# Four chained transformer layers on one core: later fp4 weights, a packed tile written twice, and a planner that counts a slow TensorE after a pause

## The chip, the cores and the metric

The kernel runs on one core of one Trainium2 chip, as a single program. The metric is the device time of that program in microseconds. Three runs of the kernel before gave 2689.86, 2690.91 and 2692.45 us, so the median is 2690.91 us.

## What is computed

The input `x` has 8 sequences of 1024 rows of 256 numbers, in float32. Four blocks follow each other, each of the form `x = x + block(layernorm(x))`:

```python
x = x + _L0_attn_ref(_layernorm(x), ...)   # linear attention with 16 heads, then a 256-1024-256 MLP with gelu
x = x + _L0_ffn_ref(_layernorm(x), ...)    # 256-1024-256 MLP with relu
x = x + _L1_attn_ref(_layernorm(x), ...)   # softmax attention, 256 wide, over the 1024 rows of a sequence
x = x + _L1_ffn_ref(_layernorm(x), ...)    # gated MLP, 704 wide
```

The last block rounds both its activations and its three weight matrices to a 4-bit grid in groups of 16:

```python
scale = jnp.maximum(jnp.max(jnp.abs(xb), axis=-1, keepdims=True) / 6.0, 1e-12)
q = _GRID[jnp.searchsorted(_MID, jnp.abs(xb / scale))] * jnp.sign(xb / scale) * scale
```

The linear attention forms running sums along the sequence (`cumsum`), sums products over the 16 numbers of a head, and multiplies vectors of 16 numbers by one number per head and position.

## The kernel before

**Tiling.** A chunk is 128 rows, a group (the code says flow) is four chunks, so a sequence has two flows and the program has 16, numbered p = 0 to 15. Each flow passes through linear attention (`linear_group`, `linear_span` at line 919, `linear_chunk` at 1079), then through the two MLPs of layer 0 (`dense`, 1269), then layernorms (`norms_1`, `norms_2`). Once both flows of a sequence are through, its eight chunks pass through softmax attention and the fp4 MLP (`soft_chunk`, 1429). Different flows are at different stages at the same time: the linear attention of flow p runs among the MLP work of flow p - 1 and the soft chunks of earlier sequences.

**Who sets the order.** Every part of the work is a Python generator that yields what it needs next. The class `Plan` (line 63) keeps a small model of the machine while the program is being written: when each engine is free, when each tile is done. `Plan.run` (267) always takes the part whose next step could start soonest, and among equals the one with the lowest due number `at`, which is counted in flows. `Plan.took` (157) charges each step a cost in this model; the TensorE cost is 1.68e-3 us per column of a matmul, and a DMA is charged at 160 GB/s on one shared `rings` time. Every instruction is recorded by the class `Queue`, whose call is line 308; so nearly all instructions of the profile have the line L308, and they are told apart by their tiles. `add_manual_dep` pins the order on each engine to the order in which the plan wrote it. Nothing is decided at run time: what the plan wrote first on an engine runs first on it.

**DMAs.** All DMAs are issued by SyncE (SP) in one order. An SP instruction whose tile isn't ready holds up all DMAs written after it. The MLP weights stream through five buffers `w_ff` of 256 KB (`W_FF = 5`, `load_weights` at 1314): one MLP step reads one buffer, with two matmuls of `half` (the first layer) and, up to two steps later, two matmuls into the accumulator (`w_ff,hidden`). The two DMAs that refill a buffer can only be issued when its last matmul is done.

**The spread.** In linear attention one number per head and position has to be multiplied into 16 rows. The numbers are packed: `flow` and later `scale` are [128, 128] tiles whose row 32 t + h holds head h at the 128 positions of chunk t. `spread` (763) writes such a tile to DRAM as `flat`, 32 rows of 512 numbers, and reads it back so that every head's row lands on 16 partitions: 4 tiles of [128, 512] for `flow`, 2 for `scale`. This is done in the flows p = 1 to 15; flow 0 works in halves and uses matmuls in its place (`spread_near`, 785). On the way back the source pattern is 8 rows, each 16 times, of 512 numbers:

```python
ap=[[GT, 8], [0, DH], [1, width]],
```

What follows the spread of `flow` on VectorE (DVE): for each of four tiles a product with `k` or `q`, a running sum (`prod<-one,carry_w,spread`) and another product. Then come the head sums on TensorE (`prod,hsum`), the division (`div`), and the packed tile `scale`, whose spread is multiplied into `q`; only then can the chunks of the flow start (`qz`).

**The fp4 weights.** `fp4_weights` (645) loads 18 pieces of the three matrices (`w_raw`), rounds each on DVE and ScalarE (ACT) with the helper `fp4` (604), transposes it on TensorE and copies it to `wgT`, `wuT` or `wdT`. Its due number is `at = 0.9 + 2.2 * i / 18` for piece i. It may start once the MLPs have begun (`count["stage"] == 4`). The soft chunks need all pieces before their first product with `wgT`.

Of the kernel before, what the change touches and what calls it, by code (L numbers as in the profile page):

```python
# [9 lines left out]
F32 = mybir.dt.float32  # L10
# [6 lines left out]
P = 128  # L17
D = 256
H = 16
DH = D // H  # L20
# [10 lines left out]
GT = G * P  # L31
# [31 lines left out]
class Plan:  # L63
# [12 lines left out]
    def __init__(self, tc, nc):  # L76
        self.tc, self.nc = tc, nc
        self.free = {}
        self.done = {}
        self.by = {}  # L80
        self.banks = []
        self.live = {}
        self.slots = {}
        self.kind = {}
        self.size = {k: v[0] for k, v in TILES.items()}
        self.spare = False
        self.used = {}
        self.held = set()
        self.kept = set()
        self.last = {}  # L90
        self.act_set = 0
        self.tiled = False
        self.parts = []
        for name in ("tensor", "vector", "scalar", "gpsimd", "sync"):
            setattr(self, name, Queue(self, name))
# [61 lines left out]
    def took(self, queue, op, args, kw):  # L157

        aps = [x for x in list(args) + list(kw.values()) if isinstance(x, bass.AP)]
        outs = [kw["out"] if "out" in kw else aps[0]]  # L160
        if kw.get("accum_out") is not None:
            outs.append(kw["accum_out"])
        size = 1
        for ap in aps:
            n = 1
            for d in ap.shape[1:]:
                n *= d
            size = max(size, n)
        after = 0.06
        if queue == "tensor":  # L170
            size = 1
            for d in outs[0].shape[1:]:
                size *= d
            cost = size * (0.84e-3 if op == "transpose" else 1.68e-3)
            tiled = op == "matmul" and (kw["lhsT"].shape[-1] <= 32 or kw["lhsT"].shape[0] <= 32)
            if tiled:
                cost *= 0.25
            if tiled != self.tiled:
                cost += 0.2
            self.tiled = tiled  # L180
            after = 0.2
        elif queue == "vector":
            each = {"reciprocal": 6.2e-3, "tensor_tensor_scan": 2.15e-3}.get(op, 1.05e-3)
            cost = 0.15 + each * size
            if op == "tensor_scalar" and outs[0].dtype == BF16:
                cost = 0.16 + 0.26e-3 * size
        elif queue == "scalar":
            cost = (0.16 if op == "copy" else 0.26) + 0.82e-3 * size
            for x in args:
                if not isinstance(x, bass.AP) and self.SETS.get(x, self.act_set) != self.act_set:  # L190
                    self.act_set = self.SETS[x]
                    cost += 1.3
        elif queue == "gpsimd":
            cost = 0.55 + 0.7e-3 * size
            if op in ("tensor_scalar", "iota"):
                cost = 0.22
            elif op == "memset":
                cost = 0.1 + 0.9e-3 * size
        else:
            cost = 0.4  # L200
        start = self.free.get(queue, 0.0)
        for ap in aps:
            name = ap.tensor.name
            if self.by.get(name) != queue:
                start = max(start, self.done.get(name, 0.0))
            if name not in self.done and name in self.held:
                start = max(start, self.used[name])
        end = start + cost
        if queue == "sync":
            n = 4e-6 / 160e-3  # L210
            for d in outs[0].shape:
                n *= d
            self.free["rings"] = max(self.free.get("rings", 0.0), end) + n
            after = self.free["rings"] - end + 1.8
        self.free[queue] = end
        for ap in outs:
            self.done[ap.tensor.name] = end + after
            self.by[ap.tensor.name] = queue
        for ap in aps:
            name = ap.tensor.name  # L220
            self.used[name] = max(self.used.get(name, 0.0), end + after)
            if queue != "tensor" and name not in self.kept:
                self.held.discard(name)
# [11 lines left out]
    def pe(self, *tiles, **kw):  # L235
        return self.need("tensor", tiles, **kw)

    def dve(self, *tiles, **kw):
        return self.need("vector", tiles, **kw)

    def act(self, *tiles, **kw):
        return self.need("scalar", tiles, **kw)

    def dma(self, *tiles, **kw):
        return self.need("sync", tiles, **kw)
# [81 lines left out]
def block_stack_kernel(ctx: ExitStack, tc: tile.TileContext, a: dict, out: bass.AP):  # L327
# [21 lines left out]
    nc, pe, dve, act, dma = plan, plan.pe, plan.dve, plan.act, plan.dma  # L349
# [9 lines left out]
    hbm = ctx.enter_context(tc.tile_pool(name="hbm", bufs=1, space=bass.MemoryType.DRAM))  # L359
# [10 lines left out]
    def tr_bank():  # L370
        return mm_bank().rearrange("p (k t) -> p k t", k=4)

    def fresh(kind, need, name=None):

        need.fresh = kind
        yield need
        return make(kind, name)
# [151 lines left out]
    for i in (1, 0):  # L529
        nc.sync.dma_start(out=wqkv[i], in_=wqkv_in[i])  # L530
        nc.sync.dma_start(
            out=bqk1[:, 2 * i : 2 * i + 2],
            in_=a[f"L0_attn_b{'qk'[i]}"].rearrange("(k p) -> p k", p=P),
# [111 lines left out]
    def fp4_weights():  # L645
        pieces = []
        for name, dstT in (("L1_ffn_w_gate", wgT), ("L1_ffn_w_up", wuT)):
            for r0, rows in INTER_TILES:
                turns = [(dstT[:, k, r0 : r0 + rows], k * P, P) for k in range(2)]
                pieces.append((a[name][r0 : r0 + rows, :], turns))  # L650
        for n in range(2):
            for c0 in range(0, INTER, D):
                width = min(D, INTER - c0)
                turns = []
                for f0 in range(0, width, P):
                    rows = min(P, width - f0)
                    dst = wdT[:rows, (c0 + f0) // P, n * P : (n + 1) * P]
                    turns.append((dst, f0, rows))
                pieces.append((a["L1_ffn_w_down"][n * P : (n + 1) * P, c0 : c0 + width], turns))
        raws = {}  # L660
        for i, (src, turns) in enumerate(pieces):
            for j in range(i, min(i + 3, len(pieces))):
                if j not in raws:
                    ahead = pieces[j][0]
                    raws[j] = (yield from fresh(
                        "soft",
                        dma(at=0.9 + 2.2 * i / len(pieces), when=lambda: count["stage"] == 4),
                        "w_raw",
                    ))[
                        : ahead.shape[0], : ahead.shape[1]  # L670
                    ]
                    nc.sync.dma_start(out=raws[j], in_=ahead)
            rows, width = src.shape
            raw = raws.pop(i)
            at = 0.9 + 2.2 * i / len(pieces)
            yield dve(raw, at=at)
            yield from fp4(raw, width, rows)
            yield pe(raw, banks=1)
            bank = tr_bank()
            for k, (dst, c0, n) in enumerate(turns):  # L680
                nc.tensor.transpose(bank[:n, k, :rows], raw[:, c0 : c0 + n], ident[:rows, :rows])
            plan.drop(raw)
            yield act(bank)
            for k, (dst, c0, n) in enumerate(turns):
                nc.scalar.copy(dst, bank[:n, k, :rows])
        weights.add("fp4")
# [76 lines left out]
    def spread(packed, tiles):  # L763


        width = packed.shape[0] // 32 * P
        flat = hbm.tile([32, GT], F32, tag="packed", name="packed", bufs=4)
        yield dma(packed)
        nc.sync.dma_start(
            out=flat[:, :width].rearrange("r (t l) -> t r l", l=P), in_=packed  # L770
        )
        out = {}
        for b in tiles:
            t = out[b] = yield from fresh("flow", dma(flat), "spread")
            nc.sync.dma_start(
                out=t[:, :width],
                in_=bass.AP(
                    tensor=flat.tensor,
                    offset=flat.offset + 8 * b * GT,
                    ap=[[GT, 8], [0, DH], [1, width]],  # L780
                ),
            )
        return out
# [22 lines left out]
    def running(out, cur, carry, b, first, last):  # L806
# [19 lines left out]
    count = {  # L826
        "halves": 0,
        "dense": 0,
        "acc": 0,
        "res": 0,  # L830
        "v": 0,
        "scored": 0,
        "attended": 0,
        "linear": 0,
# [787 lines left out]
```

## Time and profile before

| what | value |
|---|---|
| median of the runs before | 2690.91 us (2689.86 to 2692.45) |
| the profiled execution's own time | 2683.94 us |
| its span | 2682.2 us |
| mean granted TensorE clock | 0.991 |
| TensorE matmul busy (PE) | 2597.4 us, 97% of the span |
| VectorE busy (DVE) | 1969.3 us, 73% |
| ScalarE busy (ACT) | 1246.7 us, 46%, of it 308 table loads of 1283 ns |
| GpSimd busy (POOL) | 560.5 us, 21% |
| DMA | 207.00 MB in the kernel's queue, 25.9% of 16 engines |
| DMAs `packed<-flow` and `packed<-scale` | 15 and 15, 64 KB each |
| DMAs `spread<-packed` | 90, 256 KB each |

The profiled execution is 7 us shorter than the median of the timed runs; its durations and its span belong together, so sums are made against it. Times in the views are microseconds from the span's start. PE is the matmul side of TensorE, PEld its weight loads, SPq the DMA-issuing queue of SyncE. A float32 matmul has two records in the trace. In brackets behind a row stands how long the engine was idle before it, and what it waited for. In a table of windows, each engine has its busy time in that window, then come the granted share of the TensorE clock, the busy share of the core's 16 DMA engines, and what they moved.

### The profile page before, as it was taken

What the parts mean: (1) busy time and instruction counts of PE and PEld (TensorE: products, weight loads), DVE (VectorE), ACT (ScalarE), POOL (GpSimd) and SP (SyncE); (2) the same over time, 40 slices, a digit from 0 to 9 for tenths busy, and PEclk for the clock granted to TensorE, in tenths of its full rate; (3) what the DMA queues carried; (4) which work ended last, traced back from release to release, by engine and by line L of the source; (5) the groups of instructions that cost most, each with busy time, mean ns of one, the idle gap of its engine ahead of it and who ended that gap; (6) DMA issues with size and microseconds to landing.
All of it is one profiled execution on the core that took longest, in us unless ns stands there. A gap on an engine that the chain in (4) does not pass through costs nothing.

```text
span 2682.2 us, 45602 instructions
## 1 busy us (share of the span) xinstructions
PE 2597.4 (97%) x16687; PEld 2014.0 (75%) x16687; DVE 1969.3 (73%) x4514; ACT 1246.7 (46%) x2430; POOL 560.5 (21%) x1101
## 2 busy tenths in 40 slices
PE   6999999999999999999999999999999999999997
PEld 4777777777777777777777777777777777787765
DVE  8889687776858668686776858778586776856576
ACT  2443445535455453645536354363635536344343
POOL 1232232221212213122131212212121131212000
PEclk8999999999999999999999999999999999999999
DMA  3334222312223222232322223132231322322100
GB/s 87 107 105 143 89 82 64 108 59 89 73 69 106 66 86 73 69 96 71 91 73 76 80 75 106 52 92 75 70 108 54 98 63 71 89 66 81 41 12 12
DMA packets 282135, 209.92 MB, mean 78 GB/s; under 512 B 23864, under 2 KB 270392, under 8 KB 281912
## 3 DMA queue, kind: packets, MB, share of 16 engines
q1 hardware_dynamic: 281912, 207.00, 25.9%
q8 instruction: 133, 2.18, 0.3%
q14 instruction: 90, 0.74, 0.1%
HBM read 188.17 MB, written 18.74 MB: 77 GB/s over the span
## 4 chain that ended last, share of the span: by engine, by line
PE 80%; DVE 12%; DMA 2%; issue 1%; ACT 1%; POOL 1%; SPq 0%; DVEq 0%; ACTq 0%
PE bank L308 80%; DVE hid L308 2%; DVE prod L308 1%; DVE n L308 1%; DVE ln_st L308 1%; DMA spread<-packed 1%; DVE x_amax L308 1%; DVE u L308 1%; DMA w_ff<-in_L_attn_W_dram 1%; DVE res L308 1%; POOL ln_rstd L308 1%; DVE div L308 1%; DVE e L308 0%; DVE q L308 0%; DVE ln_mv L308 0%
## 5 line engine op out<-in xcount | busy, mean ns | idle before, releaser
L308 PE MATMUL bank<-half,w_ff 128*128 128x256 f32 x2048 | 533.6, 383 | 14.5 <-DMA w_ff<-in_L_ffn_w_dram 6.0
L308 PE MATMUL bank<-w_ff,hidden 128*128 128x256 f32 x2048 | 530.4, 383 | 7.7 <-issue 6.6
L308 PEld LDWEIGHTS bank<-half,w_ff 128*128 128x128 f32 x2048 | 379.4, 191 | 91.4 <-issue 26.6
L308 PEld LDWEIGHTS bank<-w_ff,hidden 128*128 128x128 f32 x2048 | 371.1, 191 | 96.0 <-issue 50.7
L308 ACT ACT_TABLE_LOAD x308 | 395.2, 1283 | 75.2 <-PE bank L308 71.1
L308 POOL TENSOR_SCALAR ln_ve<-ln_mv 128x1 f32<-128x1 f32 x384 | 96.0, 250 | 1320.7 <-DVE ln_mv L308 1299.4
L308 ACT ACTIVATE hidden<-bank,c_L_ffn_b 128x256 f32<-128x256 f32 x256 | 121.1, 473 | 338.0 <-PE bank L308 336.7
L308 PE MATMUL bank<-n2T,qT 128*128 128x512 f32 x512 | 241.4, 594 | 0.9 <-ACT qT L308 0.9
L308 POOL TENSOR_TENSOR ln_rstd<-ln_ve,neghalf 128x1 f32<-128x1 f32 x384 | 229.4, 597 | 32.0
L308 PE MATMUL bank<-vt,probT 128*128 128x256 f32 x1024 | 232.2, 380 | 0.0
L308 PEld LDWEIGHTS bank<-vt,probT 128*128 128x128 f32 x1024 | 193.2, 190 | 30.3 <-issue 3.3
L308 ACT ACTIVATE hidden<-bank,c_L_attn_b 128x256 f32<-128x256 f32 x256 | 121.4, 474 | 177.0 <-PE bank L308 175.4
L308 PE MATMUL bank<-wdT,hqT 128*128 128x256 f32 x768 | 178.0, 382 | 1.8 <-ACT hqT L308 1.8
L308 PE MATMUL bank<-wgT,xqT 128*128 128x352 f32 x512 | 173.4, 461 | 1.1 <-ACT xqT L308 0.9
L308 PE MATMUL bank<-wuT,xqT 128*128 128x352 f32 x512 | 172.4, 459 | 0.0
L308 DVE TENSOR_TENSOR sc<-bank,triu 128x512 f32<-128x512 f32 x256 | 159.4, 679 | 5.3 <-PE bank L308 3.8
L308 PEld LDWEIGHTS bank<-wdT,hqT 128*128 128x128 f32 x768 | 145.4, 191 | 22.8 <-ACT hqT L308 2.8
L308 DVE TENSOR_TENSOR hid<-hid,bank 128x352 f32<-128x352 f32 x118 | 60.9, 516 | 133.8 <-PE bank L308 92.0
L308 POOL TENSOR_TENSOR xr<-xr,b_L_attn_ln_b 128x256 f32<-128x256 f32 x64 | 49.3, 788 | 482.6 <-DMA xr<-in_L_attn_inputs_dram 482.6
L308 PEld LDWEIGHTS bank<-n2T,qT 128*128 128x128 f32 x512 | 93.6, 190 | 69.5 <-issue 62.7
L308 PEld LDWEIGHTS bank<-wuT,xqT 128*128 128x128 f32 x512 | 97.3, 190 | 54.2
L308 PEld LDWEIGHTS bank<-wgT,xqT 128*128 128x128 f32 x512 | 92.6, 190 | 37.0 <-issue 3.8
(214 smaller groups left out, 4384.4 us busy)
## 6 DMA issues: line engine op xcount, KB each, us to landing
w_ff<-in_L_attn_W_dram SPq DMA_DIRECT2D x512, 128.0 KB
w_ff<-in_L_ffn_w_dram SPq DMA_DIRECT2D x512, 128.0 KB
spread<-packed SPq DMA_DIRECT2D x90, 256.0 KB
x<-in_L_attn_inputs_dram SPq DMA_DIRECT2D x64, 128.0 KB
xr<-in_L_attn_inputs_dram SPq DMA_DIRECT2D x64, 128.0 KB
rows<-res SPq DMA_DIRECT2D x64, 128.0 KB
out_dram<-y SPq DMA_DIRECT2D x64, 128.0 KB
rows<-rows SPq DMA_DIRECT2D x56, 128.0 KB
```

The lines of the kernel that those rows point to most:

```text
L308: ins = method(*args, **kw)
```

## The change

Three edits. First, the plan's model: a TensorE step that starts more than 2.0 us after the last one ended makes TensorE cost double until 2.1 us after that start, and DMAs are charged at 250 GB/s in place of 160. Second, the fp4 weight pieces get the due numbers 1.5 to 3.0 in place of 0.9 to 3.0. Third, the packed tile is written to DRAM twice, side by side (`flat` becomes [32, 2, 512]), by two DMAs, and a spread reads 16 rows, each 8 times, in place of 8 rows, each 16 times. The tile that it fills is the same.

```diff
@@ class Plan, __init__
+        self.ran = self.slow = 0.0
@@ class Plan, took
+        if queue == "tensor":
+            if start - self.ran > 2.0:
+                self.slow = start + 2.1
+            if start < self.slow:
+                cost *= 2
+            self.ran = start + cost
         end = start + cost
         if queue == "sync":
-            n = 4e-6 / 160e-3
+            n = 4e-6 / 250e-3
@@ fp4_weights
-                        dma(at=0.9 + 2.2 * i / len(pieces), when=lambda: count["stage"] == 4),
+                        dma(at=1.5 + 1.6 * i / len(pieces), when=lambda: count["stage"] == 4),
...
-            at = 0.9 + 2.2 * i / len(pieces)
+            at = 1.5 + 1.6 * i / len(pieces)
@@ spread
-        width = packed.shape[0] // 32 * P
-        flat = hbm.tile([32, GT], F32, tag="packed", name="packed", bufs=4)
+        flat = hbm.tile([32, 2, GT], F32, tag="packed", name="packed", bufs=4)
         yield dma(packed)
-        nc.sync.dma_start(
-            out=flat[:, :width].rearrange("r (t l) -> t r l", l=P), in_=packed
-        )
+        for e in range(2):
+            nc.sync.dma_start(out=flat[:, e, :].rearrange("r (t l) -> t r l", l=P), in_=packed)
...
             nc.sync.dma_start(
-                out=t[:, :width],
+                out=t,
                 in_=bass.AP(
                     tensor=flat.tensor,
-                    offset=flat.offset + 8 * b * GT,
-                    ap=[[GT, 8], [0, DH], [1, width]],
+                    offset=flat.offset + 8 * b * 2 * GT,
+                    ap=[[GT, 16], [0, DH // 2], [1, GT]],
                 ),
             )
```

## The prediction, written before the result was known

> **What bounds the kernel now.** I read the page's busy times, then the windows of four stages, to see where TensorE isn't full.
>
> ```profile
> core 0: us, PE busy (x) PEld busy (x) DVE busy (x) ACT busy (x) POOL busy (x), PEclk, DMA share, GB/s
> 0.00:84.70 84.70, 59.15 (x472) 44.00 (x473) 68.99 (x185) 25.80 (x62) 19.06 (x50) 0.82 0.29 76
> 84.70:345.00 260.30, 242.21 (x1802) 190.72 (x1801) 214.97 (x510) 111.64 (x259) 77.83 (x143) 0.97 0.39 115
> 345.00:2414.00 2069.00, 2047.18 (x13313) 1593.58 (x13312) 1513.59 (x3425) 1002.59 (x1898) 439.15 (x853) 1.00 0.26 79
> 2414.00:2682.20 268.20, 248.82 (x1105) 185.71 (x1103) 171.75 (x397) 106.63 (x213) 24.42 (x56) 0.99 0.12 37
> ```
>
> The matmuls are the same before and after, so a change can move only TensorE's idle time and the time at a low clock. Idle are 84.7 - 59.15 = 25.6 us at the start, 260.3 - 242.2 = 18.1 us in the ramp, 21.8 us in the long middle (1%), 19.4 us at the end: 85 us in all. Next, the ramp's worst two stretches, and who ended TensorE's waits there (time line of PE, then of SP):
>
> ```profile
> 135.00 2.07 PE L308 MATMUL bank<-half,w_ff 128*128 128x256 f32 x4 [5.72 <-DMA w_ff<-in_L_ffn_w_dram]
> ...
> 230.16 2.08 PE L308 MATMUL bank<-half,w_ff 128*128 128x256 f32 x4 [4.28 <-DMA w_ff<-in_L_attn_W_dram]
> ```
>
> ```profile
> 124.48 2.52 SPq L308 DMA_DIRECT2D spread<-packed  x4
> 127.10 0.88 SPq L308 DMA_DIRECT2D xr<-in_L_attn_inputs_dram  x2
> 128.08 6.32 SPq L308 DMA_DIRECT2D w_ff<-in_L_ffn_w_dram  x6
> ...
> 221.13 2.44 SPq L308 DMA_DIRECT2D spread<-packed  x4
> 223.68 0.91 SPq L308 DMA_DIRECT2D w_ff<-in_L_attn_W_dram  x2
> ```
>
> Both pauses, 10.0 us together, are MLP weights that were issued behind the four spreads of flows 1 and 2. The first pair is issued at 128.08 and lets TensorE go at 135.00, 6.9 us later; a load in an empty queue (`xr`, at 212.10 on the chain that ended last) took 2.06 us. While only spread data is moving:
>
> ```profile
> 224.00:226.00 2.00, 1.08 (x6) 0.44 (x4) 1.90 (x5) 0.30 (x2) 0.12 (x1) 1.00 0.51 196
> ```
>
> half of the 16 DMA engines are busy and they move 196 GB/s. The pauses are followed by half clock:
>
> ```profile
> 131.60:138.40 6.80, 3.40 (x8) 2.77 (x9) 6.62 (x9) 0.47 (x1) 3.88 (x4) 0.50 0.64 159
> 227.20:234.00 6.80, 3.84 (x9) 3.14 (x10) 6.48 (x13) 0.47 (x1) 0.00 (x0) 0.50 0.55 146
> 63.40:73.40 10.00, 7.52 (x22) 5.84 (x23) 6.06 (x17) 2.69 (x7) 2.25 (x8) 0.50 0.01 2
> ```
>
> At half clock the 3.40 and 3.84 us of matmuls cost 1.7 and 1.9 us more than at full clock, the 7.52 us at 63 cost 3.8. DVE is nearly full in the first two (6.62 and 6.48 of 6.8 us). Last, a pause at the start that isn't a DMA's:
>
> ```profile
> 65.88 0.34 PE L308 MATMUL bank<-ident,scale 64*128 64x64 f32 x1 [3.35 <-DVE scale L308]
> ```
>
> **What the Trainium skill says.** "DMA: Bandwidth & Descriptors", section "Why a DMA increments its semaphore by 16 and not by 1": a DMA of this kind runs on the largest k up to 16 engines that divides the slowest dimension of both sides. The spread's source begins with 8 rows: k = 8, which agrees with the DMA share of 0.51 above; with 16 rows k = 16. The packed write begins with 4: k = 4, and stays there. "TensorE: Matmul & The Clock Gate", "Part 1: The HAM clock gate": the clock is halved after an idle window of some 3.4 us and comes back after a busy one; the trace agrees in kind (0.50 in pieces of 6.8 us), but the clock fell here only 1.3 us after the pause at 225.9 began.
>
> **The change part by part.** Sums are against the profiled execution, 2683.94 us; its span of 2682.2 is 1.7 less, and the median of the runs is 7.0 more. I carry the difference over to the median.
>
> *Spread on 16 engines.* Four spreads are 4 x 256 KB = 1.05 MB: 1.05 MB / 196 GB/s = 5.35 us before. On 16 engines at the same rate each, 2.7 us; their issue takes 2.5 us anyway. All that queues behind moves up by 2.65 us. In the built order the weights of MLP steps 16 (flow 1's spread) and 47 (flow 2's) still stand right behind the spreads, and between the first spread and their use lies as much matmul work as before (some 4.9 and 4 us), so the pauses don't vanish: 5.7 - 2.65 = 3.1 and 4.3 - 2.65 = 1.6. In flow 1 the two `xr` loads no longer stand ahead (0.88 us), one `w_raw` does (0.42): 2.6. Bounds: below, both fall to about 1 us (2.06 us landing behind the issue alone); above, nothing is gained if source rows or memory hold the spreads, not their engines.
>
> *Packed row twice.* 30 more issues at 0.57 us on SP, and the copy runs on 4 engines again. The spread waits for both, perhaps 0.9 to 1.5 us longer, and SP's weights wait behind it. The plan puts 3.0 us of matmuls between packed write and spread of flow 2 where it put 2.1, which covers most; I charge 0.4 us in each of the two places: pauses 3.0 and 2.0, gain 2.7 + 2.3 = 5.0 us. In flows 3 to 15 the spreads lie under MLP and soft-chunk matmuls: between 345 and 2414 us TensorE waited 1.9 us in all for a weight (longest 1.1), so nothing is counted there. If that cover is gone, see the third rival.
>
> *Half clock at the two pauses.* With 2 to 3 us they may stay above the point: the 2.24 us pause at 334.6 kept full clock, 3.35 us didn't. Of 1.7 + 1.9 I take 3.0.
>
> *fp4 weights later.* A piece costs DVE 0.41 + 0.17 + 0.25 + 0.42 + 0.22 + 2 x 0.42 + 0.43 = 2.7 us, 18 pieces 49 us. In the built order 9 `w_raw` instructions of DVE stand ahead of flow 1's spread where 27 did: 18 / 5 x 2.7 = 9.7 us of DVE less, and that spread comes some 8 us of matmuls earlier. This relieves the waits for a DVE `n` or `w_raw` at 145 (0.89), 160 (0.74), 221 (0.82) and 225 (0.79): of 3.2 us I take 1.5. The work lands in front of 325, where there is room: DVE is busy 22.5 of the 40 us from 285. It costs nothing there; the last transpose stands 35 us of matmuls ahead of the first product with `wgT`. The loads move on SP too, 18 issues of 0.42 us; none falls between spreads and a late weight except the one counted.
>
> *The plan's half rate.* In the built order the second half of flow 0 changes: its `prod,hsum` comes before the matmuls of chunk 1, and on DVE two `kv` products (0.48) and `u`, its statistics, `u`, `h` (about 1.9) no longer stand ahead of `e`, or do so after it. So `scale` is some 2.5 us earlier at 65.9: gain 2.5 us (bounds 1 and 3.4, the whole pause). Of the 3.8 us at half clock after it I take 0.5. The order reconverges: from flow 5 on the same steps stand within a few us of each other, and of the last 1400 TensorE rows 36 differ, so the end's 19 us stay.
>
> *Table loads.* The built order has 320 where 308 were, 12 x 1.283 = 15.4 us of ACT, which is idle over half the time. At 311 two loads in a row did cost a pause of 1.4. I charge 0.5 us in one of three, 2 us; the ends are 0 and 15.4, and reshuffled work in the middle may add 3 us either way.
>
> Sum: 5.0 + 3.0 + 1.5 + 2.5 + 0.5 - 2 = 10.5; I round up to 12, since a ramp with fewer pauses feeds the middle's 21.8 us better too. 2690.9 - 12 = 2679.
>
> **Rivals.** (1) The ramp closes: pauses to about 1 us and no half clock: 8 + 3.6 + 3.2 of waits, 3.4 + 3.8 at the start: 22 us, 2669. For it: issue takes as long as the data on 16 engines. Against it: the weights stand as close behind the spreads as before. (2) Spreads aren't held by engines, since each 2 KB row is read many times from one place: the pauses stay, table loads take back the start's gain: 2688 to 2691. For it: nothing but the doubt that 392 GB/s are to be had; against it: 0.51 at 196. This includes the change not doing what it says. (3) Slower: SP's order. Behind `packed` SP waits some 1.5 us longer, 30 times, and weights queue there. In steady flows the shortest distance from a weight's issue to its use behind a pair of spreads is 3.5 us of matmuls, against 2.06 us of landing. If the longer wait exceeds this slack by 1 us in flows 3 to 15, 13 x 2 x 1 = 26 us are lost against 12 won: 2705; it decides from 0.7 us. Against it: faster spreads shorten that same landing.
>
> **Numbers.** Chances: forecast (2673 to 2685) 0.56, ramp closes (2664 to 2672) 0.14, nothing gained (2686 to 2693) 0.20, SP slower (over 2696) 0.10. 0.2% is 5.4 us, about what a measurement of this kernel can tell from no change: faster, below 2685.5, is 0.56 + 0.14 + 0.02 = 0.72; slower 0.10; same 0.18. The range is 2664 to 2693: it leaves out the third rival and some tails.
>
> **What would show it.** Spreads: a DMA share near 1 and over 300 GB/s behind the four issues, in place of 0.51 and 196. Pauses before `half,w_ff` at flows 1 and 2 of 1 to 3 us and at most one piece of half clock after 80. `ident,scale` near 63. The middle's idle time within 4 us of 21.8. I am wrong if the pauses keep their length, if new ones stand behind `packed`, or if the middle moves more than the ramp.

## The result and the profile after

The changed kernel took 2683.17 us (median of 6 runs, 2680.7 to 2688.15) against 2691.68 us before (6 runs): ratio 0.9973, 95% interval 0.9963 to 0.9984. A second, longer comparison (21 runs against 41) gave 2683.32 against 2689.54 us, ratio 0.9976 (0.9970 to 0.9983). By the ratios the change gains 6.5 to 7.3 us (by the medians 6.2 and 8.5) of the 12 forecast.

The two profiled executions show almost none of this: 2683.53 us (span 2681.8) after, 2683.94 before. The profiled execution before was quicker than any of the 41 timed runs of its kernel. In the longer comparison the mean granted clock was 0.9906 after and 0.9892 before. By an estimate from these means, 0.0014 x 2690 = 3.8 us of the gain is time lost at half clock, which a pair of single profiles doesn't show reliably. The rest is idle time of TensorE. The windows of the four stages, after (columns as in the prediction):

```profile
core 0: us, PE busy (x) PEld busy (x) DVE busy (x) ACT busy (x) POOL busy (x), PEclk, DMA share, GB/s
0.00:84.70 84.70, 61.21 (x470) 44.87 (x471) 69.19 (x183) 25.38 (x61) 20.20 (x51) 0.80 0.29 76
84.70:345.00 260.30, 244.71 (x1816) 192.66 (x1815) 205.86 (x508) 117.64 (x266) 74.50 (x141) 0.99 0.39 113
345.00:2414.00 2069.00, 2044.74 (x13302) 1592.06 (x13301) 1524.56 (x3429) 1009.10 (x1904) 465.31 (x853) 1.00 0.28 80
2414.00:2681.80 267.80, 250.23 (x1104) 187.22 (x1103) 171.57 (x397) 106.53 (x213) 25.43 (x56) 0.99 0.12 37
```

Window less PE busy is idle time: 23.5 at the start (25.6 before), 15.6 in the ramp (18.1), 24.3 in the middle (21.8), 17.6 at the end (19.4). In all 81.0 in place of 84.9: 3.9 us less, and with the 3.8 us of clock 7.7, which is about the measured gain.

Where the ramp waits now (time line of PE, after):

```profile
65.27 0.25 PE L315 MATMUL bank<-ident,scale 64*128 64x64 f32 x1 [2.64 <-DVE scale L315]
124.66 1.10 PE L315 MATMUL bank<-half,w_ff 128*128 128x256 f32 x4 [3.15 <-DMA w_ff<-in_L_ffn_w_dram]
131.62 0.43 PE L315 MATMUL bank<-prod,hsum 128*32 128x128 f32 x8 [1.62 <-DVE prod L315]
151.70 1.17 PE L315 MATMUL bank<-qz,k 32*128 32x256 f32 x16 [2.54 <-ACT qz L315]
225.38 0.44 PE L315 MATMUL bank<-ident,w_raw 128*128 128x128 f32 x2 [2.57 <-DVE w_raw L315]
249.41 0.33 PE L315 MATMUL bank<-ident,scale 128*128 128x128 f32 x1 [2.03 <-DVE scale L315]
```

The weight pause of flow 1 fell from 5.72 to 3.15 us and that of flow 2 is gone. But in the same two flows four pauses of 1.6 to 2.6 us stand where there was none over 0.9: now DVE's work behind the spreads (`prod`, `scale`, and `qz`, which ACT makes from `q<-q,spread`) and an fp4 piece (`w_raw`) are late. And while spreads drain in flow 1 (after):

```profile
119.00:121.00 2.00, 2.00 (x12) 1.75 (x11) 1.21 (x4) 1.31 (x6) 0.04 (x1) 1.00 1.02 272
120.00:122.00 2.00, 1.51 (x8) 0.98 (x6) 1.42 (x2) 0.98 (x3) 0.00 (x0) 1.00 1.03 243
121.00:123.00 2.00, 0.51 (x3) 0.11 (x1) 1.93 (x3) 0.22 (x1) 0.00 (x0) 1.00 1.04 240
```

The share (last column but one) is 1 and more in place of 0.51: all 16 engines work. They move 240 to 272 GB/s in place of 196, not the 392 that twice the engines would give. Packets of 2 KB belong to the spreads alone, so the trace tells them apart: the first two windows hold nothing else, the third about one sixth of other data. Over all flows I took windows of 2 us, 1 and 2 us behind the first packet of four spreads, and kept those in which at least 97% of the bytes are spreads: they average 254 GB/s after (18 windows, 241 to 268) and 189 before (29 windows).

### The profile page after: what moved, and what is told of

It reads as the page before. It is cut to its first block, busy times and chain, and to the rows that moved or that the text cites. A ratio compares the mean times of both kernels' runs of the same rounds, so it can differ in the third digit from the quotient of the medians.

```text
span 2681.8 us, 45726 instructions
## 1 busy us (share of the span) xinstructions
PE 2600.9 (97%) x16687; PEld 2016.8 (75%) x16687; DVE 1971.2 (74%) x4514; ACT 1258.6 (47%) x2442; POOL 585.4 (22%) x1101
## 4 chain that ended last, share of the span: by engine, by line
PE 72%; DVE 18%; DMA 4%; ACT 2%; issue 1%; POOL 1%; SPq 0%; DVEq 0%; ACTq 0%; POOLq 0%
PE bank L315 72%; DVE prod L315 3%; DVE hid L315 2%; DMA spread<-packed 2%; DVE n L315 2%; DVE ln_st L315 1%; DVE div L315 1%; DVE u L315 1%; DVE spread L315 1%; DVE x_amax L315 1%; DVE res L315 1%; ACT L315 1%; DVE e L315 1%; DVE mx L315 1%; DVE q L315 1%
## 5 line engine op out<-in xcount | busy, mean ns | idle before, releaser
L315 PEld LDWEIGHTS bank<-half,w_ff 128*128 128x128 f32 x2048 | 380.2, 191 | 81.7 <-issue 23.9
L315 POOL TENSOR_TENSOR ln_rstd<-ln_ve,neghalf 128x1 f32<-128x1 f32 x384 | 240.8, 627 | 32.0
L315 PEld LDWEIGHTS bank<-wdT,hqT 128*128 128x128 f32 x768 | 145.4, 192 | 22.5 <-ACT hqT L315 2.8
L315 DVE TENSOR_REDUCE mx<-bank 128x1 f32<-128x512 f32 x128 | 86.7, 677 | 45.7 <-PE bank L315 45.2
```

The source lines that it names most:

```text
L315: ins = method(*args, **kw)
```

## The experiments

Theory A: the gain is the spreads on 16 engines, which shorten the weight pauses. Theory B: it is the order that the plan writes with other numbers (half rate, 250 GB/s, later fp4). Theories C and D, formed on the way, say how the two depend on each other. "Idle" below is worked out as above from each profile's four windows: start, ramp, middle, end.

| kernel | median us | ratio to before (95%) | TensorE idle by stage, us |
|---|---|---|---|
| before | 2689.4 to 2690.8, by comparison | 1 | 25.6, 18.1, 21.8, 19.4 |
| changed, again | 2683.32 | 0.9976 (0.9970 to 0.9983) | 23.7, 15.3, 24.5, 17.6 |
| changed order, 8 engines | 2705.38 | 1.0065 (1.0052 to 1.0079) | 22.6, 21.3, 28.9, 17.6 |
| order before, 16 engines | 2690.51 | 1.0004 (0.9997 to 1.0010) | 25.2, 17.8, 22.9, 19.1 |
| changed order, 8 engines, one copy | 2703.68 | 1.0054 (1.0040 to 1.0067) | 23.5, 22.1, 31.3, 17.7 |
| without later fp4 | 2683.50 | 0.9969 (0.9957 to 0.9980) | 22.3, 17.0, 20.2, 17.6 |
| without half rate | 2686.97 | 0.9984 (0.9977 to 0.9990) | 24.0, 15.0, 23.6, 19.1 |
| without 250 GB/s | 2683.57 | 0.9972 (0.9963 to 0.9981) | 22.9, 14.1, 25.3, 18.1 |
| spread alone | 2696.44 | 1.0020 (1.0013 to 1.0027) | 25.8, 13.3, 29.0, 20.7 |
| without 16 engines | 2708.02 | 1.0070 (1.0057 to 1.0084) | 22.8, 19.9, 34.5, 18.0 |
| distinct rows (other data) | 2659.51 | 0.9889 (0.9872 to 0.9906) | 22.5, 11.6, 9.9, 17.6 |
| rows 16 KB apart | 2700.07 | 1.0043 (1.0028 to 1.0059) | 22.8, 18.1, 37.0, 17.7 |
| rows 2560 bytes apart | 2681.47 | 0.9965 (0.9953 to 0.9978) | 23.3, 17.6, 23.6, 17.6 |

**The orders held fixed.** The changed kernel again:

> The changed kernel once more, as the base that the next three are held against on the same chip. All theories: about 7 us under the kernel before, ratio 0.996 to 0.9985, with the pauses of the first profile after (3.1 us before half,w_ff near 124, 2.6 near 225, 2.5 before qz near 151, 2.0 before ident,scale near 249), since the order of the work is fixed when the program is written.

As expected: ratio 0.9976, and the same pauses to within some 0.5 us. Then its order with 8 engines:

```diff
-                    ap=[[GT, 16], [0, DH // 2], [1, GT]],
+                    ap=[[2 * GT, 8], [0, DH], [1, GT]],
```

> Every engine's order is that of the changed kernel, row for row, and so are the two packed copies; only the pattern that a spread reads is 8 rows, each 16 times, again. Theory A (the gain is the 16 engines): four spreads of flow 1 take 5.35 us in place of some 4.2 us (1.05 MB at 196 and at 250 GB/s), so the pause near 124 grows from 3.1 to 4.2 us or more, the one near 225 from 2.6 to 3.7, each with a piece of half clock behind it: 2 x (1.1 + 1.8) = 5.8 us, so +4 to +8 us against the changed kernel. Theory B (the gain is the order that the plan writes, with its later fp4 weights): within 1.5 us of the changed kernel.

It cost 22 us by the medians, (1.0065 - 0.9976) x 2690 = 24 by the ratios, three times as much as expected or more, so Theory B in its plain form is out: the changed order needs quick spreads. The waits of PE for each releaser (8 engines; us in total, times, longest):

```profile
PE bank L315 <- DMA w_ff<-in_L_ffn_w_dram: 11.1, 6, 5.5
...
PE bank L315 <- DMA w_ff<-in_L_attn_W_dram: 8.7, 6, 3.3
```

19.8 us for weights, where the changed kernel, again, has 5.8:

```profile
PE bank L315 <- DMA w_ff<-in_L_ffn_w_dram: 4.2, 2, 3.2
...
PE bank L315 <- DMA w_ff<-in_L_attn_W_dram: 1.6, 3, 0.9
```

Over half of the 8-engine waits lie in the steady flows (10.9 us between 345 and 2414), where the prediction counted nothing; for example this one, with half clock around it (time line of PE, then a window, 8 engines):

```profile
1492.74 2.08 PE L315 MATMUL bank<-half,w_ff 128*128 128x256 f32 x4 [2.90 <-DMA w_ff<-in_L_attn_W_dram]
...
1491.90:1498.70 6.80, 5.96 (x13) 4.00 (x14) 6.52 (x12) 2.49 (x4) 0.00 (x0) 0.50 0.16 46
```

The longer waits are only part of the loss. Idle time in all rose from 81.1 to 90.4 us; the mean granted clock fell from 0.9906 to 0.9862, and 0.0044 x 2690 = 11.8 us is more than half of the loss (an estimate from these means). And the loss isn't the price of the engines alone. This edit also puts the 8 rows of a spread 4 KB apart, where they lie 2 KB apart in the kernel before, and they come more slowly (windows while spreads drain in flow 1, 8 engines):

```profile
117.00:119.00 2.00, 1.92 (x10) 1.36 (x8) 0.28 (x2) 1.16 (x3) 0.00 (x0) 1.00 0.57 173
118.00:120.00 2.00, 0.92 (x5) 0.47 (x3) 1.04 (x2) 0.47 (x1) 0.00 (x0) 1.00 0.59 170
```

The kernel before moved 196 GB/s on as many engines. The four spreads of a flow take 7.5 us here from the first packet to the last (median of 15 flows), 6.6 in the kernel before and 4.7 in the changed kernel, again. A run further down takes the 16 engines away with the rows 2 KB apart.

The order of before with 16 engines: the new `spread` in the kernel before, with the plan not counting the second copy:

```diff
         for e in range(2):
+            plan.mute = e == 1
             nc.sync.dma_start(out=flat[:, e, :].rearrange("r (t l) -> t r l", l=P), in_=packed)
+        plan.mute = False
@@ class Plan, took
+        if self.mute:
+            return
```

> The order of the kernel before on every engine, with the 16-row pattern; the second packed copy is written, but the plan doesn't count it, so nothing else moves. Theory A: the pauses of 5.7 and 4.3 us fall by 1 to 1.2 us less some 0.5 us for the second copy, so to 5.1 and 3.7 us, still with half clock: -1 to -3 us against the kernel before; if the spreads ran at 392 GB/s, as the prediction took, the pauses would fall to 3 and 2 us and the time by 6 to 8 us. Theory B: within 1.5 us of the kernel before.

In time it is within 0.1% of the kernel before (Theory B's number), though its weight pauses shrank by more than Theory A said for 250 GB/s (time line of PE):

```profile
133.28 2.08 PE L311 MATMUL bank<-half,w_ff 128*128 128x256 f32 x4 [3.48 <-DMA w_ff<-in_L_ffn_w_dram]
...
229.10 2.08 PE L311 MATMUL bank<-half,w_ff 128*128 128x256 f32 x4 [3.36 <-DMA w_ff<-in_L_attn_W_dram]
```

10.0 us became 6.8, but the ramp's idle time fell by 0.3 only: the time came back as other waits (over the whole run those for DVE `prod` went from 9.1 to 11.9 us, for `v` from 2.5 to 3.7, for ACT `prob` from 5.9 to 6.8), and the middle lost 1.1. In this order the 16 engines, together with the second copy that comes with them, are worth nothing measurable.

One packed copy, 8 engines, in the changed order (the plan counts the missing copy):

```diff
         for e in range(2):
-            nc.sync.dma_start(out=flat[:, e, :].rearrange("r (t l) -> t r l", l=P), in_=packed)
+            half_ = dict(out=flat[:, e, :].rearrange("r (t l) -> t r l", l=P), in_=packed)
+            if e == 0:
+                nc.sync.dma_start(**half_)
+            else:
+                plan.took("sync", "dma_start", (), half_)
```

> The changed kernel's order, 8 engines for a spread as in the run with 8 engines, and the second packed copy isn't written though the plan counts it. Beside that run it prices the second copy: if a copy costs its issue (0.57 us) and about as much landing on its four engines, the spreads of flows 1 and 2 start 0.6 to 1.2 us earlier and the time falls by 1 to 3 us against that run; if the copy lies beside the wait for the first, by less than 0.5 us.

1.0054 against 1.0065: 3 us less, with intervals that overlap, and its profile shows no less idle time (94.6 against 90.4 us in all). The price of the second copy is not resolved.

**One edit taken out, the plan left to write its order.**

```diff
-at=1.5 + 1.6 * i / len(pieces)
+at=0.9 + 2.2 * i / len(pieces)
```

> The changed kernel with the fp4 weights due from 0.9 again. By the prediction's price the later fp4 weights are worth 1.5 us (waits for a DVE n or w_raw at 145 to 225), plus what it counted for the spread that comes earlier: +1.5 to +4 us against the changed kernel. Rival: only the match between spreads and the plan's DMA rate matters; within 1 us.

0.9969 against 0.9976, with intervals that overlap: the later fp4 weights give nothing that can be measured, as the rival had it. Without them TensorE waited 14.3 us for DVE `n`, with them 11.8 us for `n` and 3.8 for `w_raw`.

```diff
-            if start - self.ran > 2.0:
-                self.slow = start + 2.1
-            if start < self.slow:
-                cost *= 2
-            self.ran = start + cost
```

> The changed kernel without the plan's doubled TensorE cost behind pauses. The prediction gave that model 3 us at the start (scale 2.5 us earlier, 0.5 of half clock); the trace after shows the pause before ident,scale only 0.7 us shorter and at the start no less time lost in all (37.5 us against 37.3). So I expect 0 to +2 us against the changed kernel; if the model also serves the later flows, +4 or more.

0.9984 against 0.9976, about 2 us slower, in line with the expectation's upper end; but the intervals overlap by a little, so a loss isn't shown, and the profiles differ by only 0.7 us of idle time in all (81.7 against 81.0). Two pauses do come back. The one before `ident,scale` is 3.3 us again, 0.7 more, though the idle time of the whole start is 24.0 against 23.5 and 23.7. The other is at the very end (time line of PE, without half rate):

```profile
2677.25 1.45 PE L308 MATMUL bank<-ident,q 128*128 128x128 f32 x6 [2.33 <-DVE q L308]
```

In the changed kernel:

```profile
2674.37 0.85 PE L315 MATMUL bank<-ident,q 128*128 128x128 f32 x6 [0.60 <-DVE q L315]
```

It goes with the place of one row of DVE. Time line of DVE, without half rate:

```profile
2672.63 0.89 DVE L308 TENSOR_TENSOR q<-q,q_c 128x704 f32<-128x704 f32 x1
2674.95 0.42 DVE L308 TENSOR_TENSOR y<-bank,x 128x256 f32<-128x256 f32 x1 [1.43 <-PE bank L308]
2675.30 0.88 DVE L308 TENSOR_TENSOR q<-q,q_c 128x704 f32<-128x704 f32 x1
```

and after:

```profile
2671.48 1.82 DVE L315 TENSOR_TENSOR q<-q,q_c 128x704 f32<-128x704 f32 x2
2673.33 0.89 DVE L315 TENSOR_TENSOR q<-q,x_s 128x704 f32<-128x704 f32 x1
2674.14 0.42 DVE L315 TENSOR_TENSOR y<-bank,x 128x256 f32<-128x256 f32 x1
```

Without half rate, as in the kernel before, `y` stands between two steps of the last `q` and makes DVE wait for a product (1.43 us here, 1.07 before); after, it stands behind `q`.

```diff
-            n = 4e-6 / 250e-3
+            n = 4e-6 / 160e-3
```

> The changed kernel with the plan charging DMAs at 160 GB/s again; spreads still on 16 engines. Theory C (a plan that believes in faster DMAs writes an order that needs them; it is that order which fails on 8 engines, by 22 us, and that gains on 16): +4 to +8 us, so the whole gain is gone, as in the order of the kernel before. Theory A (16 engines give the gain whatever the plan believes): within 2 us of the changed kernel.

0.9972: Theory C in this form, that the belief in 250 GB/s makes the order, falls. Then the spread alone on the kernel before:

> The kernel before with the 16-row spread and two copies alone, and the plan left to count the second copy. Theory A: -3 to -7 us against the kernel before. Theory C: within 2.5 us of the kernel before, as with its order kept by hand (ratio 1.0004), since the plan still places the weights for 160 GB/s.

Its edit is the `spread` part of the change, alone. It is slower than before, 1.0020: no theory had that. Theory A's place is right, the whole isn't. The weight pauses of flows 1 and 2 are 2.5 and 1.6 us and the ramp's idle time falls by 4.8 us; the middle gives back 7.2 and the end 1.3. Waits in the middle, us in total (spread alone):

```profile
PE bank L308 <- DVE v L308: 12.4, 12, 1.9
PE bank L308 <- DVE res L308: 4.3, 4, 2.6
```

The kernel before waited there 2.5 us for `v`. From the run with the order of before and 16 engines (1.0004) this one differs only in that the plan counts the 30 second copies. So it is the order that the plan wrote for them, mostly that of the middle, that costs about 4 us.

The opposite, the changed kernel with the `spread` of before:

> The changed kernel without its spread: one packed copy, 8 engines, and an order that the plan writes for that, with the half rate, the 250 GB/s and the later fp4 weights. Theory D (the other edits make an order that leans on quick spreads, as the run of the changed order on 8 engines showed with +22 us): slower than the kernel before, +8 to +15 us, mostly in waits for w_ff (20 us in all against 12). Rival: the model and the fp4 edit give the gain by themselves, -3 to -7 us, and the changed order failed on 8 engines only because it had been written around a second copy.

1.0070: Theory D holds, and more strongly than expected. Without 16 engines the other edits make a kernel 19 us slower than before; 23.7 us are waits for weights, 16.3 of them in the middle (waits of PE between 345 and 2414, without 16 engines):

```profile
PE bank L315 <- DMA w_ff<-in_L_ffn_w_dram: 10.3, 9, 2.4
...
PE bank L315 <- DMA w_ff<-in_L_attn_W_dram: 6.0, 4, 3.6
```

Here 10.4 us of the loss is idle time (95.3 against 84.9 in all); the granted clock is 0.9865 against 0.9890 of the kernel before beside it, 0.0025 x 2690 = 6.7 us (an estimate from these means).

Four kernels now stand against each other, each in the order that the plan writes for it: before 1, the new spread alone 1.0020, the other edits alone 1.0070, both 0.9976. Each half by itself loses; together they gain. Which of the other edits the spread needs stays open: later fp4 weights, half rate and 250 GB/s were each taken out singly, and none of the three shows a clear loss.

**What holds 16 engines near 250 GB/s.** All in the changed kernel's order:

```diff
-                    tensor=flat.tensor,
-                    offset=flat.offset + 8 * b * 2 * GT,
-                    ap=[[GT, 16], [0, DH // 2], [1, GT]],
+                    tensor=a["L0_attn_inputs"].tensor,
+                    offset=a["L0_attn_inputs"].offset + b * P * GT,
+                    ap=[[8 * GT, 16], [GT, 8], [1, GT]],
```

> The changed kernel, but each spread reads 128 different rows of 2 KB of the input in place of 16 rows, each 8 times; so the multiplied values are left out (other data stand in their place), and a spread doesn't wait for the packed copies any more. Read is the rate while only spreads move. If the repeated rows are what holds the 16 engines at 250 GB/s: over 300 GB/s at a share near 1, a 2 KB row in some 100 ns in place of 135. If it is a limit of 16 engines with 2 KB rows, whatever they read: 250 again. The time is some us lower than that of the changed kernel in both cases, as the wait for packed is gone.

Windows in which only spreads move, in flows 1 and 2, distinct rows:

```profile
116.00:118.00 2.00, 2.00 (x12) 1.74 (x11) 1.90 (x5) 1.31 (x6) 0.07 (x1) 1.00 1.01 300
214.00:216.00 2.00, 1.42 (x10) 1.06 (x9) 1.52 (x4) 1.20 (x4) 1.77 (x3) 1.00 0.99 267
```

and in the changed kernel, in flow 2:

```profile
222.00:224.00 2.00, 0.81 (x4) 0.38 (x2) 1.97 (x3) 0.36 (x1) 0.20 (x1) 1.00 1.04 280
```

In flow 1 distinct rows are faster, in flow 2 they aren't. Over all flows, windows of spread data chosen as above average 295 GB/s with distinct rows (17 windows, 229 to 335) against 254 with repeated ones, and a packet of 2 KB takes 101 ns on average against 119. So reading the same rows again costs something like a seventh of the rate; it isn't what keeps 16 engines from 392, which distinct rows don't reach either. The same run shows 340 GB/s two to three microseconds later in flow 1, but there two thirds and more of the bytes are MLP and fp4 weights.

The kernel falls to 2659.5 us; most of it is in the middle, whose idle time goes from 24.3 to 9.9 us. How much of that is the rate and how much the dropped wait for the packed copies isn't told apart by this run. The rate's part looks small: the four spreads of a flow take 4.4 us from first packet to last (median of 15 flows), against 4.6 in the changed kernel. Their issue is shorter too, 0.43 us each against 0.59.

```diff
-        flat = hbm.tile([32, 2, GT], F32, tag="packed", name="packed", bufs=4)
+        flat = hbm.tile([32, 2, 8 * GT], F32, tag="packed", name="packed", bufs=4)
...
-                    offset=flat.offset + 8 * b * 2 * GT,
-                    ap=[[GT, 16], [0, DH // 2], [1, GT]],
+                    offset=flat.offset + 8 * b * 2 * 8 * GT,
+                    ap=[[8 * GT, 16], [0, DH // 2], [1, GT]],
```

> The changed kernel with its 64 packed rows 16 KB apart in DRAM in place of 2 KB. Nothing else differs. If rows that lie close together hold the spreads at 250 GB/s: over 300 GB/s and the two weight pauses each some 0.7 us shorter, -2 to -4 us against the changed kernel. If it is the repetition, or 16 engines as such: 250 again and within 1.5 us.

Neither: 18 us slower than the changed kernel (1.0043 against 0.9976). Windows in which only spreads move, in flow 1:

```profile
118.00:120.00 2.00, 1.33 (x7) 0.83 (x5) 0.10 (x1) 0.80 (x3) 0.00 (x0) 1.00 0.83 173
119.00:121.00 2.00, 0.34 (x2) 0.00 (x0) 1.07 (x2) 0.04 (x1) 0.00 (x0) 1.00 0.88 199
```

Where the repeated rows lie in DRAM matters, and 16 KB apart is worse than 2 KB. Last, the same edit with `GT + P` in place of `8 * GT`:

> The changed kernel with its packed rows 2560 bytes apart in DRAM, so that they don't all start at a multiple of 2 KB. Nothing else differs. Rows 16 KB apart cost 17 us, other rows each time gave 340 GB/s and more: so where the repeated rows lie decides how fast they are read. If a power of two between the rows is what makes them collide: over 300 GB/s behind the issue of the spreads of flow 1, DVE's waits for spreads well under 35 us in all, and -4 to -10 us against the changed kernel. If 2 KB apart is as good as a repeated read gets: 250 GB/s or less again, and 0 to +6 us.

267 and 277 GB/s at a share of 1.04 and 0.97 where only spreads move (windows 119:121 and 118:120), and 36.2 us of DVE waits for spreads against 35.0: as with 2 KB. The 340 GB/s that this expectation starts from is the figure that was mostly weights. The ratio, 0.9965 (0.9953 to 0.9978), is the lowest of the kernels that do the whole work, but overlaps the changed kernel's interval; it isn't shown to be better. Why rows 16 KB apart are slow stays open.

## Why the prediction was right or wrong

**Sign and order of size were right; the sum was not made of the right parts.** By idle time the prediction had -2.5 at the start, -6.5 in the ramp (5.0 and 1.5), about +2 in the middle and 0 at the end. Measured: -2.1, -2.5, +2.5, -1.8. Of half clock it took 3.5 us; the mean clock over many runs says 3.8, though the profile after has two pieces of 3.4 us between 80 and 345, right behind the pauses at 225 and 249, where I allowed one, and the second profile has four (at 131.7, 152.2, 227.3 and 251.2 us). Where in the run the clock gains stays open. The two pieces of the first profile:

```profile
225.80:229.20 3.40, 3.31 (x9) 2.67 (x9) 3.30 (x9) 0.91 (x3) 0.00 (x0) 0.51 0.56 161
249.70:253.10 3.40, 3.40 (x11) 2.56 (x10) 2.63 (x9) 0.27 (x1) 1.51 (x2) 0.51 0.26 80
```

That the total fell inside the range is in part luck: the ramp gave 4 us less than forecast, the end and the start's other edits gave what wasn't forecast. Of the prediction's own signs, the spreads' 300 GB/s and the single piece of half clock failed, and the middle moved as much as the ramp (2.5 us each), the edge of what it named as being wrong.

**The rate (a term mis-sized).** "On 16 engines at the same rate each, 2.7 us": the four spreads of flows 1 and 2 took 4.6 and 4.2 us from first packet to last after (4.8 and 4.7 in the second profile). But before they took 7.4 and 6.4, not 5.35, so they are 1.7 to 2.8 us shorter and the 2.65 of the prediction came near by luck: both lengths were too small. The Trainium skill ("DMA: Bandwidth & Descriptors", as cited in the prediction) gave the number of engines, and the share of 1.03 agrees; that twice the engines give twice the rate was mine. The second rival's doubt, that rows read many times from one place hold the spreads, was true for a small part.

**"Both pauses ... fall" (right), "gain 5.0" (wrong).** 3.0 us was forecast for flow 1's weight pause, 3.15 came; 2.0 for flow 2's, which is gone. With the spread alone the ramp gained 4.8. In the changed kernel only 2.5 was kept, because the step didn't say what is late next: DVE's chain behind the spread, `prod`, `scale`, `qz`, and an fp4 piece, 1.6 to 2.6 us each. This is the step that failed.

**"In flows 3 to 15 ... nothing is counted there" (wrong).** The kernel before waited 1.9 us for weights there because its order left room. The changed order leaves less: on 8 engines it waits 10.9 us for weights in the middle. With spreads on distinct rows, not waiting for packed, the middle's idle time falls by 14.4 us, of which only some 2 were waits for weights; most were waits for DVE (`v` from 6.7 to 1.2 us). The third rival looked at the right place, weights late behind spreads in steady flows, but for another reason, the wait behind `packed`; what the runs on 8 engines show is longer spreads.

**Half rate.** Priced 2.5 + 0.5 at the start; about 2 us in all by the run without it, which that run doesn't separate from nothing. The pause at `ident,scale` accounts for 0.7 us: there `e` comes 1.2 us earlier, but DVE does `u`, `h` and two `kv` between `e` and `div`. That the whole start gained 2.1 us, near the 2.5, was luck: without half rate 1.6 of it remain, and what made them stays open. "The end's 19 us stay" failed: one of the few rows that differ there was the `y` between the steps of the last `q`, 1.7 us of pause.

**fp4 later** was priced at 1.5 us and gives nothing measurable; the waits for `n` that it removes come back as waits for `w_raw`, whose pieces now share DVE with flow 2's spreads. **The second copy**, charged 0.8 us, isn't resolved. **Table loads**: the middle did lose 2.5 us, but to waits for DVE `v` (6.5 us in place of 2.5), ACT `prob` (5.4 in place of none), DVE `scale` and `prod`, while 11 us of waits for issue and `n2T` went; that the loads cause any of it isn't shown. **Rounding up by 1.5** had no ground.

## What to carry to other kernels

The worth of a faster transfer is not a number of its own when a planner writes the order: here 16 engines gave nothing measurable in the old order, the new spread alone lost 5 us, the other edits alone lost 19, and together they gained 6.5. Price a faster transfer by the waits in the order that will be built, stage by stage, and name for each shortened wait what arrives next behind it. Take the rate of more DMA engines from a trace in which as many read the same kind of source, and before reading a rate off a window, ask whose bytes move in it.

## What wasn't expected of the hardware

Twice the engines gave 1.3 times the rate here (254 against 189 GB/s on average), and where the repeated rows lie in DRAM changes it. In windows with spread data alone, on 16 engines: rows 2 KB apart read 8 times 254 GB/s, rows 16 KB apart 205 (28 windows, 140 to 289), 128 distinct rows 295. On 8 engines: rows 2 KB apart 189, rows 4 KB apart 157 (11 windows, 114 to 187).

A pause doesn't decide by its length alone whether half clock follows. The same program, the same place, behind the pause before `qz` (2.54 us in the first profile after):

```profile
152.30:155.50 3.20, 3.20 (x26) 2.54 (x19) 3.13 (x8) 1.30 (x5) 0.74 (x2) 1.00 0.00 0
```

and in the second one, where the pause was shorter, 2.20 us:

```profile
152.30:155.50 3.20, 3.20 (x12) 2.45 (x9) 3.17 (x7) 0.89 (x4) 0.74 (x2) 0.50 0.00 0
```

The Trainium skill ("TensorE: Matmul & The Clock Gate", "Part 1: The HAM clock gate") says that the clock follows the activity in windows that run freely, so which pauses cost half clock would depend on where the windows lie in that run. That fits these two lines. The traces show such a grid: in the first profile after, the clock changes at 65.42, 225.84, 229.26, 249.74 and 253.15 us, and the later four lie 47, 48, 54 and 55 steps of 3.413 us behind the first. The idle window of some 3.4 us that the prediction cited needn't be idle throughout, though: half clock followed here on pauses of 2.03 and 2.57 us. The windows would also explain why runs of one kernel differ: runs of the changed kernel at a granted clock of 0.989 took 2686.7 us on average (3 runs), at 0.992 2679.8 us (6 runs).
